# Routed experts of a decoder: the last row puts one per tile step, row loads 9 tiles ahead, and no order between the two

## The chip, the cores and the metric

The kernel runs on one core of a Trainium2 chip. A core has TensorE (PE in the profile; its weight loads are listed apart as PEld), VectorE (DVE), ScalarE (ACT), GpSimd (POOL) and SyncE (SP), each with a queue of its own that it works off in order, and 16 DMA engines that all of them share. The metric is the device time of one execution in microseconds (us).

## The reference

Two decoder layers over 16 sequences of 256 tokens with 128 features, all in float32. Each layer is self-attention, cross-attention to a context of 64 rows per sequence, and a mixture of experts. The change concerns the mixture of layer 0:

```python
logits = xn @ router_w
probs = jax.nn.softmax(logits, axis=-1)
topv, topi = jax.lax.top_k(probs, K)
topv = topv / jnp.sum(topv, axis=-1, keepdims=True)
comb = jnp.sum(jax.nn.one_hot(topi, E, dtype=xn.dtype) * topv[..., None], axis=1)
out = jnp.zeros_like(xf)
for e in range(E):
    out = out + comb[:, e:e + 1] * _swiglu(xn, gate_up_w[e], down_w[e])
out = out + _swiglu(xn, shared_gate_up_w, shared_down_w)
```

There are 4096 tokens, E = 8 experts and K = 2 choices per token. `xn` is the layernormed input. An expert is `silu(clip(gate)) * up @ down` with a hidden width of 512.

## The kernel before, in words

**Rows.** The kernel computes only the two experts that a token has chosen. The 4096 tokens are handled as 8 chunks of 512 (four blocks of 128). When the router has chosen for a chunk, every token gets two slots in a table of rows in device memory, `rows_in`, in which each expert has a region of its own. `p_pos` (L817) works the slots out on VectorE and writes them to `slot_in` (L826). `p_put` (L828) then scatters 128 rows of 130 numbers with one indirect DMA from POOL's queue (L830): two per block, eight per chunk, 64 in all.

**Tiles.** The experts' work is done in 71 tiles of 128 rows (NTILE). Of these, 41 (EARLY) are known to be full from the counts of the first six chunks alone (EARLY_C = 6); their table `tab_a` is made as soon as chunk 5 is routed. The other 30 come from `tab_b`, which is made when chunk 7 is routed. A tile needs its rows (`fetch`, L1313, a DMA from SP's queue into one of ROWS_AHEAD buffers `xr`), its expert's gate and up weights (`weights`, L1323, 512 KB from ACT's queue), a transpose on TensorE (`turn`, L1337) and its copy on ScalarE (`turned`, L1341), the matmuls `g` and `u` (`hidden`, L1369, eight lines each in the profile), a clip on VectorE and a silu on ScalarE (`gated`, L1376 and L1377), a product (`product`, L1381), the matmuls `y` (`down`, L1387, eight lines), a copy (L1396), and an indirect DMA from POOL that scatters the results to `rows_out` (`store`, L1397).

**Order.** Layer 0's self-attention comes first, as 134 steps (`steps`), two to an iteration of its loop. The cross-attention and the routing of each chunk (`front_pieces`, L601) are cut into small pieces, and `plan` (L1079) hangs piece k of chunk c on step 16c + 22 + k. A piece is a part for TensorE and a part for the other engines. The pieces of chunks 6 and 7 reach beyond step 134 and are worked off in the loop over tiles, where step 134 + i is tile step i: chunk 6's slots are made in tile step 7, chunk 7's in step 23. In a tile step i the program emits, in this order: the weights of tile i+6, the rows of tile i + ROWS_AHEAD, one of 20 weight loads for later layers (`pending`, L1428, from step 4 on), `turn(i+1)`, `hidden(i)`, TensorE's parts of the pieces, `down(i-2)`, `turned(i+1)`, `gated(i)`, the pieces' other parts, `targets(i)`, `product(i)` and `store(i-2)`.

In the attention the order on TensorE, VectorE, ScalarE and POOL is the order written in the program; the puts of chunks 0 to 5 have places there (`put_at`, L1119 on). In the loop over tiles it is written for TensorE, VectorE, ScalarE and SP:

```python
with tc.manual_schedule(engines=ordered | {mybir.EngineType.SP}):
```

POOL is not in that set: a planner puts POOL's instructions in an order by when it reckons that they are ready, the earlier emitted one first.

**Who waits for whom.** Puts and loads go to the same table `rows_in`, and a load's address is known only at run time, so a load waits for every put emitted before it, and a put waits for every load emitted before it, unless the program declares that two of them do not depend on each other. It does so for puts among themselves. One piece of a chunk's list, at L906, emits all eight puts of chunks 6 and 7 in one step, and is empty for the others:

```python
(None, lambda: None if c < EARLY_C else [p_put(t) for t in range(TPC)]),
```

Of the kernel before, what the change touches and what calls it, by code (L numbers as in the profile page):

```python
# [22 lines left out]
P = 128  # L23
# [4 lines left out]
NCHUNK = T // CH  # L28
TPC = CH // P
# [3 lines left out]
NTILE = 2 * NT + E - 1  # L33


EARLY_C = 6
SHARED_LATE = (4, 5, 6, 7)
EARLY = -(-(2 * CH * EARLY_C - E * (P - 1)) // P)
LATE = NTILE - EARLY
# [24 lines left out]
def kernel(ctx: ExitStack, tc: tile.TileContext, a: dict, out: bass.AP):  # L64
    nc = tc.nc
# [31 lines left out]
    rows_in = tc.dram_tile([ROWS, W], F32, name="rows_in")  # L97
# [129 lines left out]
    slots = ctx.enter_context(tc.tile_pool(name="slots", bufs=1))  # L227
# [16 lines left out]
    with ExitStack() as ph:  # L244
# [319 lines left out]
        first = wpool.tile([P, E], F32, tag="first", name="first")  # L564
# [5 lines left out]
        full = fp.tile([P, E, T // P], F32, tag="full", name="full")  # L570
        tiles = fp.tile([P, EARLY, E], F32, tag="tiles", name="tiles")
# [5 lines left out]
        tab_a = fp.tile([1, 2, EARLY], I32, tag="tab_a", name="tab_a")  # L577
        tab_b = fp.tile([1, 2, LATE], I32, tag="tab_b", name="tab_b")
        puts, puts_of, tabled, room = [], {}, {}, {"m": ps_m}

        def front_constants():

# [43 lines left out]
        def front_pieces(c):  # L626
# [142 lines left out]
            def p_turned2():  # L769
                if c in SHARED_LATE and "pool" in late:  # L770
                    g["xT"] = shared_xT[c] = late["pool"].tile(
                        [P, CH], F32, tag=f"xT{c}", name=f"xT_{c}"
                    )
                else:
                    held("xT", (P, CH))
                nc.scalar.activation(g["xT"], g.pop("tp"), AF.Identity, bias=bet, scale=gam)
                if c in SHARED_LATE and "pool" not in late:
                    shared_rows[c] = tc.dram_tile([P, CH], F32, name=f"xT_rows_{c}")
                    nc.sync.dma_start(shared_rows[c], g["xT"])
# [48 lines left out]
            def p_put(t, ks=(0, 1)):  # L828
                for k in ks:
                    put = nc.gpsimd.indirect_dma_start(  # L830
                        out=rows_in,
                        out_offset=bass.IndirectOffsetOnAxis(
                            slot_in[:, k, t0 + t : t0 + t + 1], 0
                        ),
                        in_=g["xn2"][:, t, :], in_offset=None,
                    )
                    for other in puts:
                        tc.declare_no_dep(
                            put.ins, other.ins, reason="slots of tokens are all different"
                        )  # L840
                    puts.append(put)


            def mm_sgate():
# [29 lines left out]
            def p_sdown():  # L874
# [28 lines left out]
            puts_of[c] = [lambda t=t, k=k: p_put(t, (k,)) for t in range(TPC) for k in range(2)]  # L903
            return [
                *first_part,
                (None, lambda: None if c < EARLY_C else [p_put(t) for t in range(TPC)]),  # L906
                *([] if c in SHARED_LATE else [
                    (mm_sgate, p_sgate),
                    (mm_sup, p_sup),
# [7 lines left out]
        def mm_counts(tiles_seen):  # L917
            ps = tabled["ps"] = room["m"].tile(
                [P, E], F32, tag="m", name=f"counts_{tiles_seen}"
            )  # L920
            nc.tensor.matmul(ps, ones, seen[:, tiles_seen, :], start=True, stop=True)
# [57 lines left out]
        def early_pieces():  # L979
# [13 lines left out]

            return [(lambda: mm_counts(EARLY_C * TPC), table), (None, table2)]

# [31 lines left out]
        with tc.manual_schedule(engines=ordered | {mybir.EngineType.Pool}):  # L1027
# [32 lines left out]
            got = [first_stats(t0) for t0 in (0, 2)]  # L1060
# [16 lines left out]
            side = {}  # L1077

            def plan(first, pieces):  # L1079
                for k, piece in enumerate(pieces):  # L1080
                    side.setdefault(first + k, []).append(piece)

            plan(17, [(lambda h=h: ctx_turn(h), lambda h=h: ctx_turned(h)) for h in range(2)])
            for c in range(NCHUNK):
                first_step = 16 * c + 22
                plan(first_step, front_pieces(c))
                if c == EARLY_C - 1:
                    plan(first_step + 24, early_pieces())
                if c == NCHUNK - 1:
                    plan(first_step + 25, late_pieces())  # L1090
# [7 lines left out]
            steps = n + 6  # L1098
# [7 lines left out]
            put_at = {}  # L1106
            for c in range(EARLY_C):
                for j, put in enumerate(puts_of[c]):
                    step = 8 * c + 23 + (j if c < EARLY_C - 1 else j // 4)
                    put_at.setdefault(step, []).append(put)  # L1110
# [189 lines left out]
    with ExitStack() as ph:  # L1300
# [4 lines left out]

        state, stores = {}, []
        room["m"] = ps_m
        AHEAD, ROWS_AHEAD = 8, 13

        def entry(i):  # L1310
            return (tab_a, i) if i < EARLY else (tab_b, i - EARLY)

        def fetch(i):  # L1313
            tab, k = entry(i)
            r = nc.values_load(
                tab[0:1, 1, k : k + 1], engines=[mybir.EngineType.SP], min_val=0,
                max_val=ROWS - P,
            )
            xr = fp.tile([P, W], F32, tag="xr", name=f"xr_{i}", bufs=ROWS_AHEAD)
            nc.sync.dma_start(xr, rows_in[bass.ds(r, P), :])  # L1320
            state.setdefault(i, {})["xr"] = xr

        def weights(i):  # L1323
# [86 lines left out]

        plan(steps + EARLY + 4, [(None, piece) for piece in strip_pieces()])
        plan(steps + NTILE, [(None, both)])
        assert 16 * (NCHUNK - 1) + 22 + 28 - steps <= EARLY - ROWS_AHEAD and max(side) - steps <= NTILE
        with tc.manual_schedule(engines=ordered | {mybir.EngineType.SP}):
            for i in range(AHEAD - 1):
                weights(i)
            for i in range(ROWS_AHEAD):
                fetch(i)
# [137 lines left out]
    with ExitStack() as ph:  # L1556
# [230 lines left out]
        with tc.manual_schedule(engines=ordered):  # L1787
# [55 lines left out]
            def shared_sum(c):  # L1843
                nc.gpsimd.tensor_tensor(x[c], x[c], shared_of.pop(("y", c)), ALU.add)
# [46 lines left out]
            plan = [w.split(":") for w in PLAN.split()]  # L1891
            plan = [(tok, int(lag)) for tok, lag in plan]
# [50 lines left out]
    with ExitStack() as ph:  # L1943
# [289 lines left out]
        plan = [part.split(":") for part in PLAN.split()]  # L2233
        with tc.manual_schedule(engines=ordered | {mybir.EngineType.Pool}):
            for word in (
# [6 lines left out]
                part, c = word.split(":")  # L2242
# [5 lines left out]
            for word in (  # L2248
# [12 lines left out]
                part, c = word.split(":")  # L2261
# [60 lines left out]
```

## Time and profile before

| What | Value |
|---|---|
| time, median of 5 runs | 1408.45 us (1406.52 to 1409.42) |
| the profiled execution's own time | 1410.43 us |
| its span, first to last instruction | 1408.5 us |
| mean granted TensorE clock | 0.981 |
| stage of the tiles | about 566 to 820 us |
| puts of rows (L830) | 64, of which 16 in the tile stage, from 621.2 to 692.0 us |
| stores of results (L1397) | 71, median 957 ns each on POOL |
| row loads (L1320) | 71, 65 KB each; the first 13 are issued from 575.75 us on, 1.13 us apart |

How to read it. The page gives one profiled execution. "Busy" is the share of the span in which an engine executes; instructions that only wait, branch, load a register or issue a DMA are not counted, except that POOL's indirect DMAs are shown for the time in which POOL prepares them, not for the transfer. In an order of time a line is: start, duration, engine, line of the kernel, operation, output <- inputs, shape, count, and in brackets how long the engine had been idle before and what ended that. "Issue" means that the engine waited for nothing that the profile shows; "remote", that the release came from something that the profile can't place. Times in the text without a unit are us from the start of the span. The granted clock is the share of full speed that TensorE's throttle gave.

### The profile page before, as it was taken

The numbers are of one execution on the slowest core, as the hardware profiler recorded it, in microseconds if no ns is written. First come the engines' busy times: TensorE is split into PE (matmuls) and PEld (weight loads), VectorE is DVE, ScalarE is ACT, GpSimd is POOL, SyncE is SP. The second block draws the span as 40 slices with busy tenths as digits, with TensorE's granted clock in tenths as the row PEclk, the third lists the DMA queues.
The fourth block names the chain that finished last, engine by engine and source line by source line (L and its number), as shares of the span: only waits on it lengthen the run. The fifth ranks groups of instructions, "written<-read, shape, count | busy, mean of one in ns | idle before, by whom it ended". The sixth has DMA issues, their size and how long they took to land.

```text
span 1408.5 us, 37939 instructions
## 1 busy us (share of the span) xinstructions
PE 1340.9 (95%) x13205; PEld 1002.7 (71%) x13205; DVE 1108.2 (79%) x4483; ACT 942.6 (67%) x2532; POOL 733.6 (52%) x1153
## 2 busy tenths in 40 slices
PE   9999999999999999899899989999999987899998
PEld 7777777777777776689799966666666654566665
DVE  5776877777777778657678769999999977888874
ACT  6776767667676766344233349999999984776662
POOL 6463648475756656643433373553334315677651
PEclk9999999999999999999899999999999998999998
DMA  6773000000000000557577420000000000122122
GB/s 161 233 243 86 2 6 9 9 9 9 7 11 7 17 9 23 174 178 236 177 244 233 162 77 17 17 17 10 17 3 2 2 2 1 32 54 61 39 59 63
DMA packets 80349, 95.86 MB, mean 68 GB/s; under 512 B 19568, under 2 KB 62832, under 8 KB 80160
## 3 DMA queue, kind: packets, MB, share of 16 engines
q1 hardware_dynamic: 65328, 46.25, 12.1%
q10 hardware_dynamic: 10512, 38.28, 8.0%
q0 software_dynamic: 4320, 8.92, 1.9%
q8 instruction: 106, 1.74, 0.5%
q14 instruction: 83, 0.68, 0.2%
HBM read 64.24 MB, written 29.17 MB: 66 GB/s over the span
## 4 chain that ended last, share of the span: by engine, by line
PE 66%; ACT 17%; DVE 10%; issue 3%; DMA 2%; POOL 1%; SPq 0%; POOLq 0%; ACTq 0%; DVEq 0%
ACT p L1730 8%; PE pqk L414 8%; PE o L546 5%; PE s L469 5%; PE u L1369 4%; PE g L1369 4%; PE y L446 4%; PE y L1387 4%; PE t L524 4%; PE pv L431 3%; PE t L1748 3%; PE o L1772 2%; ACT pT L1759 2%; PE s L1708 2%; PE g L2149 2%
## 5 line engine op out<-in xcount | busy, mean ns | idle before, releaser
L508 POOL TENSOR_SCALAR p<-p,rs 128x128 f32<-128x128 f32 (+1 forms) x512 | 213.4, 431 | 166.4 <-DVE rs L502 124.4
L494 ACT ACTIVATE p<-p,nm 128x128 f32<-128x128 f32 (+1 forms) x512 | 226.4, 447 | 24.7 <-DVE nm L482 20.6
L1730 ACT ACTIVATE p<-p,nm 128x256 f32<-128x256 f32 x512 | 220.7, 507 | 1.7 <-DVE nm L1719 0.4
L1719 DVE CUSTOM_DVE_ANT_0 p<-s,strip 128x256 f32<-128x256 f32 x512 | 186.7, 419 | 15.2 <-PE s L1708 14.5
L533 DVE COPY pT<-t 128x384 f32<-128x384 f32 x256 | 130.1, 549 | 39.2 <-PE t L524 37.7
L482 DVE CUSTOM_DVE_ANT_0 p<-s,strip 128x128 f32<-128x128 f32 (+1 forms) x512 | 154.0, 347 | 0.5 <-PE s L469 0.2
L1397 POOL DMA_INDIRECT rows_out<-yr,to x71 | 68.4, 964 | 121.5 <-DVE yr L1396 115.6
L1748 PEld LDWEIGHTS t<-ident,p 64*128 64x128 f32 x2048 | 80.4, 140 | 54.5 <-issue 16.1
L546 PEld LDWEIGHTS o<-pT,v 128*64 128x64 f32 x1024 | 64.2, 138 | 66.4 <-issue 34.1
L425 ACT ACTIVATE k<-pqk 128x512 f32<-128x512 f32 x64 | 38.1, 596 | 108.2 <-PE pqk L414 108.2
L1748 PE MATMUL t<-ident,p 64*128 64x64 f32 x2048 | 102.9, 232 | 7.9 <-ACT pT L1759 2.4
L1377 ACT ACTIVATE gs<-gs 128x512 f32<-128x512 f32 x71 | 44.7, 630 | 88.0 <-DVE gs L1376 76.6
L469 PE MATMUL s<-k,q 64*128 64x128 f32 (+1 forms) x1024 | 100.4, 332 | 0.3 <-DVE nm L482 0.3
L546 PE MATMUL o<-pT,v 128*64 128x256 f32 (+1 forms) x1024 | 99.0, 335 | 0.6 <-DVE pT L533 0.6
L494 ACT ACTIVATION_READ_ACCUMULATOR p<-p,nm 128x1 f32 x512 | 98.1, 192 | 0.0
L524 PE MATMUL t<-ident,p 64*128 64x64 f32 x1536 | 81.6, 228 | 14.0 <-ACT pre L737 4.7
L524 PEld LDWEIGHTS t<-ident,p 64*128 64x128 f32 x1536 | 68.5, 139 | 35.7 <-POOL p L508 8.7
L1708 PE MATMUL s<-k,q 32*128 32x256 f32 x1024 | 86.8, 410 | 1.4 <-DVE nm L1719 1.4
L1759 ACT COPY pT<-t 128x512 f32<-128x512 f32 x144 | 81.1, 587 | 6.8 <-PE t L1748 5.9
L440 DVE COPY v<-pv 128x512 f32<-128x512 f32 x64 | 44.2, 690 | 50.6 <-PE o L546 28.0
L1369 PE MATMUL u<-xTs,gu 128*128 128x128 f32 x568 | 77.9, 279 | 5.0 <-issue 5.0
L1387 PE MATMUL y<-dn,hT 128*128 x568 | 77.6, 280 | 3.0 <-issue 1.9
(365 smaller groups left out, 3355.0 us busy)
## 6 DMA issues: line engine op xcount, KB each, us to landing
gu<-in_L_ffn_gate_up_w ACTq DMA_DIRECT2D x71, 512.0 KB
rows_in<-zero SPq DMA_DIRECT2D x131, 130.0 KB
spread<-wrows SPq DMA_DIRECT2D x16, 512.0 KB
xr<-rows_in SPq DMA_DIRECT2D x71, 65.0 KB
y<-rows_out SPq DMA_DIRECT2D x16, 256.0 KB
out_x<-yo SPq DMA_DIRECT2D x16, 128.0 KB
x<-in_x SPq DMA_DIRECT2D x7, 256.0 KB
rows_out<-yr,to POOLq DMA_INDIRECT x71
```

The costliest lines, as they stand in the source:

```text
L469: nc.tensor.matmul(ps_of[b, h][:, cols], q[rows, u2, iq], k[rows, u2, 0:nk], start=True, stop=True,)
L482: nc.vector.tensor_tensor_reduce(out=pr[:, cols], in0=ps[:, cols], in1=strip[:, h, P : 2 * P] if it == 0 else strip[:, h, :], scale=1.0, s ...
L494: nc.scalar.activation(pr[:, cols], pr[:, cols], AF.Exp, bias=nm[:, it : it + 1], scale=-1.0, accum_out=sm[:, it : it + 1],)
L508: nc.gpsimd.tensor_scalar(pr[:, cols], pr[:, cols], rs[:, it : it + 1], 1.0, ALU.mult, ALU.mult)
L524: nc.tensor.transpose(halves[r][:, i, blk, :], pr[rows, blk * P : (blk + 1) * P], ident[rows, rows],)
L533: nc.vector.tensor_copy(pT_of[u][:, :, :, r, :], tp_of[u][r])
L546: nc.tensor.matmul(po[rows, c0:N], v[:, jt, h % 8 * DH : (h % 8 + 1) * DH], pT[:, 0:N] if jt == 0 else pT[:, N:], start=(jt == 0), stop=(j ...
L1369: nc.tensor.matmul(ps[:, f, :], gu[:, lo + f * P : lo + (f + 1) * P], xT, start=True, stop=True,)
L1387: nc.tensor.matmul(ps, s["hT"][:, f, :], dn0[:, bass.ds(s["e"], 1), f, :].rearrange("p e d -> p (e d)"), start=(f == 0), stop=(f == NF0 - 1),)
L1719: nc.vector.tensor_tensor_reduce(out=pr[:, it, :], in0=ps[:, it, :], in1=strip1[:, h, (1 - it) * P : (1 - it) * P + N], scale=1.0, scalar= ...
L1730: nc.scalar.activation(pr[:, it, :], pr[:, it, :], AF.Exp, bias=nm[:, it : it + 1], scale=-1.0)
L1748: nc.tensor.transpose(halves[r][:, k, jt, it, :], pr[rows, it, jt * P : (jt + 1) * P], ident[rows, rows],)
```

## The change

Four edits, all around the rows of layer 0's experts. The piece that emitted a chunk's eight puts at once is taken out of the list. For chunks 6 and 7 the eight puts are planned one per step instead, behind the chunk's last piece: tile steps 8 to 15 and 24 to 31. For chunks 0 to 3 the piece was empty; with it gone, their three pieces of the shared expert come one step earlier. Rows are loaded 9 tiles ahead, not 13, so there are 9 buffers `xr`. And each load of an early tile (i < EARLY) and each put of chunks 6 and 7 are declared not to depend on each other, whichever is emitted first. The assertion now asks that the last put is emitted before the first load that still depends on it, that of tile 41.

```diff
@@ p_put
                     puts.append(put)
+                    if c >= EARLY_C:
+                        late_puts.append(put)
+                        for other in early_fetches:
+                            tc.declare_no_dep(
+                                put.ins, other.ins, reason=APART,
+                            )
@@ front_pieces
             return [
                 *first_part,
-                (None, lambda: None if c < EARLY_C else [p_put(t) for t in range(TPC)]),
                 *([] if c in SHARED_LATE else [
@@ the plan
-                plan(first_step, front_pieces(c))
+                front = front_pieces(c)
+                plan(first_step, front)
+                if c >= EARLY_C:
+                    plan(first_step + len(front), [(None, put) for put in puts_of[c]])
+                    last_put = first_step + len(front) + len(puts_of[c]) - 1
@@ the tiles
-        AHEAD, ROWS_AHEAD = 8, 13
+        AHEAD, ROWS_AHEAD = 8, 9
@@ fetch
-            nc.sync.dma_start(xr, rows_in[bass.ds(r, P), :])
+            got = nc.sync.dma_start(xr, rows_in[bass.ds(r, P), :])
+            if i < EARLY:
+                early_fetches.append(got)
+                for other in late_puts:
+                    tc.declare_no_dep(got.ins, other.ins, reason=APART)
@@ the loop over tiles
-        assert 16 * (NCHUNK - 1) + 22 + 28 - steps <= EARLY - ROWS_AHEAD and max(side) - steps <= NTILE
+        assert last_put + 1 - steps <= EARLY - ROWS_AHEAD and max(side) - steps <= NTILE
```

`APART` is the reason given: the tiles of the first table are full of rows of the chunks that it counts, and rows of later chunks have slots behind those.

More of the change, by code (lines that the diff above doesn't have):

```diff
@@ L36 @@
 EARLY_C = 6
+APART = (
+    "the tiles of the first table are full of rows of the chunks that it counts, and rows of later"
+    " chunks have slots behind those"
+)
 SHARED_LATE = (4, 5, 6, 7)
@@ L579 @@
         puts, puts_of, tabled, room = [], {}, {}, {"m": ps_m}
+        late_puts, early_fetches = [], []
         def front_constants():
@@ L841, in p_put @@
                     puts.append(put)
+                    if c >= EARLY_C:
[3 more added lines that the diff above has]
+                                put.ins, other.ins, reason=APART,
+                            )
             def mm_sgate():
```

## The prediction

> **What bounds the kernel now.** I read the page first (who is busy, which slices lose clock), then busy time by stretches over the stage of the experts' tiles (566 to 820 us), then the order of time of POOL and of TensorE where a stretch falls out, then the waits there.
>
> ```profile
> span 1408.5 us, 37939 instructions
> PE 1340.9 (95%) x13205; PEld 1002.7 (71%) x13205; DVE 1108.2 (79%) x4483; ACT 942.6 (67%) x2532; POOL 733.6 (52%) x1153
> ```
>
> TensorE is busy 95% of the span: time is to be had only where it is not. Stretches of the tile stage (columns: length, busy us of PE, PEld, DVE, ACT, POOL, granted clock, DMA share, GB/s):
>
> ```profile
> 620.00:640.00 20.00, 16.65 (x106) 14.17 (x106) 7.66 (x23) 5.97 (x11) 11.81 (x13) 0.83 0.49 151
> 640.00:660.00 20.00, 20.00 (x182) 20.00 (x181) 17.19 (x56) 9.18 (x19) 9.34 (x11) 1.00 0.81 250
> 680.00:702.00 22.00, 15.39 (x105) 13.99 (x104) 12.59 (x49) 4.32 (x9) 11.59 (x12) 0.77 0.46 144
> 702.00:722.00 20.00, 20.00 (x181) 20.00 (x181) 15.35 (x46) 8.01 (x15) 7.62 (x8) 1.00 0.78 251
> ```
>
> Two stretches are bad: 106 matmuls where 182 go, clock at 0.83 and 0.77, and the DMA engines idler than beside them. What they have in common is POOL's queue (order of time, first stretch):
>
> ```profile
> 619.08 0.96 POOL L1397 DMA_INDIRECT rows_out<-yr,to  x1 [1.21 <-DVE yr L1396]
> 621.20 0.96 POOL L830 DMA_INDIRECT rows_in<-xn,slot_in  x1 [1.15 <-DMA xr<-rows_in]
> 622.46 0.95 POOL L830 DMA_INDIRECT rows_in<-xn,slot_in  x1 [0.30 <-issue]
> ...
> 630.03 0.96 POOL L830 DMA_INDIRECT rows_in<-xn,slot_in  x1 [0.30 <-issue]
> 631.29 0.96 POOL L1397 DMA_INDIRECT rows_out<-yr,to  x1 [0.30 <-issue]
> 632.55 0.96 POOL L1397 DMA_INDIRECT rows_out<-yr,to  x1 [0.30 <-issue]
> ```
>
> The eight puts (L830) stand back to back, one every 1.26 us, once the first has waited for a row load; the stores they held up (L1397) follow at the same pace. From 682.10 to 695.78 it is eight puts and three stores. TensorE in that second burst:
>
> ```profile
> 687.21 0.27 PE L1337 MATMUL xTr<-ident,xr 128*128 128x128 f32 x1
> 689.08 1.22 PE L1369 MATMUL g<-xTs,gu 128*128 128x128 f32 x8 [1.60 <-issue]
> 691.35 0.37 PE L1369 MATMUL u<-xTs,gu 128*128 128x128 f32 x1 [1.05 <-issue]
> 692.05 0.37 PE L1369 MATMUL u<-xTs,gu 128*128 128x128 f32 x1 [0.33 <-issue]
> 693.47 0.37 PE L1369 MATMUL u<-xTs,gu 128*128 128x128 f32 x1 [1.04 <-issue]
> ...
> 700.01 0.42 PE L1337 MATMUL xTr<-ident,xr 128*128 128x128 f32 x1
> ```
>
> The matmuls of `u` have their operands and need no one, yet they come 0.7 or 1.4 us apart (eight take 1.06 us elsewhere). The others wait for TensorE though it has done its part:
>
> ```profile
> ACT gs L1377 <- DVE gs L1376: 28.5, 13, 9.4
> DVE gs L1376 <- remote: 13.7, 2, 8.3
> ACT xTs L1341 <- remote: 5.7, 1, 5.7
> ```
>
> "Remote" is a release that the profile can't place: the clip of `g` starts at 635.40 and 697.72, while the `g` it reads ended at 625.93 and 685.59. So in a dense burst TensorE's signals come late, then its own issue slows down. Both times everything is released 1.9 us after the burst's last indirect DMA ends (633.51 and 695.78). That the dense run is the cause is my reading; the rows show only that they coincide, and that nothing like it stands elsewhere: stores 2.18 us apart (700.35, 702.53, 704.72) harm nothing.
>
> **What the two bursts cost.** From transpose to transpose (L1337) a tile step is 2.79 us. In burst 1 the transposes are at 624.77 and 635.95: 11.18 us, of which 2.79 is the step and 3.2 the gate's matmuls of chunk 7 (626.66 to 629.9), so 5.2 are lost; the next step, at half clock, takes 4.62, so 1.8 more. Burst 2: 687.21 to 700.01 is 12.80, so 10.0 lost, and 3.37 for the next, 0.6 more. Sum 7.0 + 10.6 = 17.6 us. No single step can give more than about that.
>
> **The change, part by part.**
>
> *Puts apart (L906 goes, L1086 adds them).* The number stays: 16 indirect DMAs, 0.96 us each and 0.30 between. What moves is their place on POOL's queue. POOL is not among the engines whose order is written out in this stage: what is ready early goes first there. The norm of chunk 7 (L670), emitted in step 7, ran at 610.67, ahead of the store of step 6 at 613.89; the two mixes (L742, L750) of steps 12 and 13 ran at 637.80 and 639.04 ahead of the store of step 11. So eight puts emitted over eight steps need not run over eight steps.
>
> *Puts and early loads don't wait for each other (declared).* In the old order it was this wait that held the puts to 621.20 and 682.10. Their slots are written by
>
> ```profile
> L826 DVE CAST slot_in<-slot x2: 170/170/171, 615.1 to 674.3; 128x8 int32<-128x8 f32 x2
> ```
>
> so all eight can go from 615.3 and 674.5. Between two stores (2.79 us apart, 1.26 each) stands 1.53 us of free POOL: room for one put, or for two with the store late. I take two per step as likeliest: put, put, store is 3.78 us of POOL in a step of 2.79, dense again, but every third operation is now a store that needs a result of TensorE. When signals lag, POOL meets a store that is not ready and pauses, and the pause ends the lag. The lag begins with the third or fourth dense operation (VectorE's L715 waits until 626.15 for a matmul that ended at 623.84). Eight puts and four or five stores give two such pauses; a pause lets go 1.9 us after the last operation, and with a matmul group restarted at part clock I put 2 to 3 us of TensorE on it: an estimate, 5 us per burst, 10 in all of the 17.6. Gain 7.6. Ends: all 17.6 gone; or the whole dense run charged (rival 3), 7.3 lost. I take the middle since the order is between the two rows it is nearest to, the burst (1.26 us apart) and the stores (2.18).
>
> The wait of SP's row load for the puts goes too (its issue stood from 617.99 to 633.22). It cost nothing: the row loaded then is read at 664.2.
>
> *Rows 9 tiles ahead, not 13.* Load i is issued when tile i-9 frees its buffer and read 8 steps on, 22.3 us; the load issued at 633.22 landed by 634.63, 1.4 us. At the start four loads of 1.13 us leave SP's head; tile 9 is read at 614.4, its buffer comes free at 592. Zero; if it were late, each us would be a us of TensorE. The first load that still waits for the late puts is tile 41's, in step 32, for a put issued in step 31 at the latest; SP's wait ended 3.2 us after the last put began (630.03 to 633.22), against 22.3. Behind it on SP stand only more row loads: the 20 weight loads of `pending` are out by step 23. Zero.
>
> *Puts ahead of chunk 7's mixes on POOL.* L742 and L750 (1.27 us each) may stand behind two indirect DMAs, 2.5 us, and VectorE waits for them in order. In the old order L742 waited idle 4.3 us for ScalarE, so I book 0, with 2.5 as the bad end.
>
> *The empty piece that goes for chunks 0 to 3.* Their shared expert's three pieces come one step earlier in the attention. Same matmuls (1.1 us for `sg`); now they cost a wait of 0.24 us (L524 at 272.84 for the clip L851), and a wait of 0.69 stands beside them for the gate's evacuation (286.05). Between -4 x 0.24 and +4 x 0.69 = -1.0 to +2.8; I take 0, as the next chunk's pieces that they now meet are lighter in one step and heavier in the other.
>
> **Row against rule.** The row says that a burst of indirect DMAs holds TensorE. The Trainium skill, page SBUF — State Buffer, section "SBUF: two separate sides", says that a DMA cannot be slowed by a compute operation or the other way round, the one trap being descriptors that GpSimd can't write while VectorE holds a shared port. By that rule the puts' spacing gives nothing and the time stays 1408.5. In this trace the puts keep their 1.26 us, so that trap is not what is seen, and TensorE does slow down beside them; I go by the row.
>
> **Sum.** The profiled execution took 1410.43 us, span 1408.5 and 1.93 around it; it lies 1.98 above the median 1408.45 (1406.52 to 1409.42). 1410.43 - 7.6 = 1402.8; against the median, 1400.9. **Predicted 1401 us**, 1396.5 to 1405.5 for this case alone.
>
> **Rivals.**
> 1. *One put per step, as emitted.* Store and put are 2.52 us of 2.79, POOL pauses in each step. For it: the pair at 640.46 and 641.75 harmed nothing (the clip at 641.77 follows `g` at 641.73, steps stay 2.79). Against: POOL's habit of running what is ready. Loss left about 2: gain 15.6, 1393.
> 2. *The burst only moves.* All eight are ready at once, and if nothing is ready between them they run back to back from 615.3 and 674.5, six to eight us earlier. Then the loss is as now, 17.6 give or take 3: 1405.5 to 1411.4. That TensorE's stall has another cause gives the same.
> 3. *Slower: no pauses.* If the stores are always ready when POOL comes to them, 8 puts and 5 stores run dense for 13 x 1.26 + 1.9 = 18.3 us. In burst 2 10.6 of 15.6 us were lost, 68%; of 18.3 that is 12.4, twice 24.9 against 17.6: +7.3, 1415.8. It decides from where TensorE's results lie a full store ahead of POOL through the burst. Against it: in burst 2 the store after the backlog waited 4.56 us for its result (700.35).
>
> **How the numbers follow.** Main case 0.35, rival 1 0.27, rival 2 0.20, rival 3 0.18. 0.2% is 2.8 us, about what a measurement of this kernel can tell from no change: faster means below 1405.6. Faster takes the main case but a little, and rival 1: 0.60; same is nearly all of rival 2: 0.19; slower is rival 3 and rival 2's upper end: 0.21. The range 1392 to 1412 leaves out the best of rival 1 and most of rival 3.
>
> **What would show it.** Right: L830 no longer in runs of eight but broken by L1397; granted clock above 0.9 and some 150 or more matmuls per 20 us where it was 106; the "remote" waits of L1376 under 3 us; no wait of L1337 for `xr`. Rival 1: no clock below 1.00 after 600 us. Rival 2: eight L830 in a row from 615 and 675. Rival 3: L830 and L1397 mixed with 0.30 between all, and transposes over 10 us apart. Wrong altogether: TensorE's slow issue at the same place without a dense run on POOL.

## The result and the profile after

| | time, median | ratio to before, 95% interval |
|---|---|---|
| before | 1410.06 us (1403.89 to 1414.20, 70 runs) | |
| after | 1412.26 us (1411.20 to 1415.86, 38 runs) | 1.0019 [1.0013, 1.0025] |

The change made the kernel slower by 0.19%, some 2.7 us: little, but clear of no change by the interval, where a gain of 7.6 us had been predicted. The profiled execution has a span of 1412.6 us against 1408.5, at the same mean clock (0.981).

The same stretches of the tile stage as in the prediction, in the kernel after (length, busy us of PE, PEld, DVE, ACT, POOL, granted clock, DMA share, GB/s):

```profile
620.00:640.00 20.00, 14.46 (x82) 12.27 (x82) 7.22 (x22) 6.36 (x10) 9.63 (x11) 0.74 0.51 141
640.00:660.00 20.00, 20.00 (x172) 18.95 (x171) 14.64 (x46) 7.62 (x14) 9.64 (x10) 1.00 0.64 200
680.00:702.00 22.00, 15.98 (x103) 14.62 (x103) 13.16 (x52) 4.81 (x9) 11.52 (x12) 0.77 0.51 162
```

Both holes are still there. The first is deeper (82 matmuls where it was 106, clock 0.74 where it was 0.83), the second is the same (103 and 105 matmuls). POOL in order of time shows why. L835 is the put, L1415 the store:

```profile
617.79 0.97 POOL L835 DMA_INDIRECT rows_in<-xn,slot_in  x1 [0.58 <-DVE at L1365]
...
620.34 0.96 POOL L835 DMA_INDIRECT rows_in<-xn,slot_in  x1 [0.30 <-issue]
621.60 0.96 POOL L1415 DMA_INDIRECT rows_out<-yr,to  x1 [0.30 <-issue]
622.87 0.96 POOL L835 DMA_INDIRECT rows_in<-xn,slot_in  x1 [0.30 <-issue]
...
627.93 0.96 POOL L1415 DMA_INDIRECT rows_out<-yr,to  x1 [0.31 <-issue]
629.20 0.95 POOL L835 DMA_INDIRECT rows_in<-xn,slot_in  x1 [0.30 <-issue]
633.94 0.96 POOL L1415 DMA_INDIRECT rows_out<-yr,to  x1 [3.79 <-DVE yr L1414]
```

Three puts, a store, four puts, a store, a put: ten operations, one every 1.26 us, with no pause. The two stores in the middle had their results before POOL reached them (0.30 of idle time, "issue"); the only pause (3.79) stands behind the last put. VectorE made these two results early in the burst:

```profile
618.59 0.28 DVE L1414 COPY yr<-y 128x128 f32<-128x128 f32 x1
620.77 0.28 DVE L1414 COPY yr<-y 128x128 f32<-128x128 f32 x1
```

The second burst has the same order from 680.62 to 692.96. TensorE's waits in it look as they did before (order of time):

```profile
686.30 0.36 PE L1387 MATMUL u<-xTs,gu 128*128 128x128 f32 x1 [0.28 <-issue]
687.72 0.27 PE L1387 MATMUL u<-xTs,gu 128*128 128x128 f32 x1 [1.06 <-issue]
...
693.33 0.37 PE L1405 MATMUL y<-dn,hT 128*128 x1 [1.03 <-issue]
694.76 0.45 PE L1355 MATMUL xTr<-ident,xr 128*128 128x128 f32 x1 [1.05 <-issue]
```

**Where the 4.1 us of the profiled span came from.** I set the start of every attention iteration and of every tile's transpose against the same one of before. The attention loses 0.57 to 0.66 us in each of chunks 0 to 3, where the shared expert's pieces moved up by a step, 2.2 us together at the first transpose. Burst 1 loses 3.1 more than it did (steps of 11.86 and 7.81 us where they were 11.18 and 4.62), burst 2 0.1 more, and 1.4 come back later. (Two later profiles of the changed kernel, in sets C and D below, show 1.6 more in burst 1 and 0.5 and 0.6 less in burst 2: 1.0 for both together, where it is 3.2 here.) The attention's loss is this wait, TensorE's flips (`t`) in chunk 0, in order of time, after:

```profile
200.19 0.27 PE L528 MATMUL t<-ident,p 64*128 64x64 f32 x1
201.34 0.58 PE L528 MATMUL t<-ident,p 64*128 64x64 f32 x11 [0.88 <-DVE gs L875]
```

and before:

```profile
199.30 0.27 PE L524 MATMUL t<-ident,p 64*128 64x64 f32 x1
199.81 0.58 PE L524 MATMUL t<-ident,p 64*128 64x64 f32 x11 [0.24 <-DVE gs L851]
```

The flips waited 0.24 us for the shared expert's clip; now the next piece (`su`) meets them, and they wait 0.88 us for its evacuation (L875): 0.64 us, four times. (Two line numbers in the description of the kernel before are off: `front_pieces` begins at L626, `put_at` at L1106.)

### The profile page after: what moved, and what is told of

It is laid out like the page before. It is cut to its first block, busy times and chain, and to the rows that moved or that the text cites. A ratio compares the mean times of both kernels' runs of the same rounds, so it can differ in the third digit from the quotient of the medians.

```text
span 1412.6 us, 37948 instructions
## 1 busy us (share of the span) xinstructions
PE 1343.1 (95%) x13205; PEld 1005.1 (71%) x13205; DVE 1108.0 (78%) x4483; ACT 943.0 (67%) x2532; POOL 736.9 (52%) x1153
## 4 chain that ended last, share of the span: by engine, by line
PE 68%; ACT 17%; DVE 11%; issue 2%; POOL 2%; DMA 1%; POOLq 0%; ACTq 0%; SPq 0%; DVEq 0%
ACT p L1748 8%; PE pqk L418 7%; PE s L473 5%; PE o L550 5%; PE g L1387 5%; PE u L1387 5%; PE y L1405 5%; PE y L450 4%; PE t L528 4%; PE t L1766 3%; PE pv L435 3%; PE o L1790 2%; PE s L1726 2%; ACT pT L1777 2%; PE g L2167 2%
## 5 line engine op out<-in xcount | busy, mean ns | idle before, releaser
L498 ACT ACTIVATE p<-p,nm 128x128 f32<-128x128 f32 (+1 forms) x512 | 226.5, 447 | 24.4 <-DVE nm L486 19.9
L1737 DVE CUSTOM_DVE_ANT_0 p<-s,strip 128x256 f32<-128x256 f32 x512 | 186.8, 419 | 15.7 <-PE s L1726 14.2
L1415 POOL DMA_INDIRECT rows_out<-yr,to x71 | 68.6, 966 | 124.9 <-DVE yr L1414 119.3
```

Of the source, the lines that this page charges most:

```text
L498: nc.scalar.activation(pr[:, cols], pr[:, cols], AF.Exp, bias=nm[:, it : it + 1], scale=-1.0, accum_out=sm[:, it : it + 1],)
L1737: nc.vector.tensor_tensor_reduce(out=pr[:, it, :], in0=ps[:, it, :], in1=strip1[:, h, (1 - it) * P : (1 - it) * P + N], scale=1.0, scalar= ...
```

## The experiments

There are five sets of runs. Each set ran on one chip, with runs of the kernel before beside it, and each on another chip. It turned out that the sets differ: before took 1410.9, 1410.9 and 1409.2 us in the sets called A, C and D here, and 1398.0 and 1399.5 us in B and E; the first table is like A, C and D. No chip had two of these sets, so whether the chip makes the difference, or something else that differed between the sets, is not shown. All ratios are within a set.

**Theories at the start.** *Density*: four or more indirect DMAs back to back on POOL hold TensorE, wherever they stand; the change moved them without thinning them out, and the empty piece adds 2.3 us. *Place*: TensorE stalls at chunk 6's and 7's late pieces for a reason of its own, and the DMAs only coincide.

### Set A: the empty piece, and the puts thinned out or gone

*The empty piece put back*, the rest of the change kept:

```diff
                 *first_part,
                 *([] if c in SHARED_LATE else [
+                    (None, lambda: None),
                     (mm_sgate, p_sgate),
```

> The changed kernel with the empty piece put back for chunks 0 to 3, so that the shared expert's pieces stand where they stood; puts, row loads and declarations as changed. Theory 'shift': the 2.2 us by which the first transpose of the tile stage is later (589.7 against 587.5) come from these pieces alone, 0.64 us in each of four chunks. Then the attention's iterations lie on those of before, and the time falls by 2.2 to 2.6 us against the changed kernel, to about 1410, the same as before. Rival 'POOL or row loads': the attention stays 2.2 us late, 1412.

Measured: 1409.67 us, ratio 0.9988 [0.9978, 0.9999]. Every attention iteration starts within 0.06 us of its time before: the shift is the whole of that loss. Both stalls stand: the tile stage is 2.5 us longer than before's.

*Each late put tied to its own tile step.* VectorE copies the put's slots in the put's step, so POOL can't run it earlier:

```diff
+                    where = slot_in[:, k, t0 + t : t0 + t + 1]
+                    if c >= EARLY_C:
+                        now = fp.tile([P, 1], I32, tag="now", name=f"now_{c}_{t}_{k}", bufs=8)
+                        nc.vector.tensor_copy(now, where)
+                        where = now[:, 0:1]
...
-                        out_offset=bass.IndirectOffsetOnAxis(
-                            slot_in[:, k, t0 + t : t0 + t + 1], 0
-                        ),
+                        out_offset=bass.IndirectOffsetOnAxis(where, 0),
```

> As the run with the piece back, and in addition each late put takes its slots from a small copy that VectorE makes in the put's own tile step (16 copies more, about 0.17 us each on VectorE, which is not the bound). So POOL's order is put, store, put, store, one put per step. Theory 'density': runs of indirect DMAs 1.26 us apart are what holds TensorE; without them no transpose comes over 5 us after the one before except in the step with the gate's matmuls (6.0), the granted clock stays 1.00 from 600 to 800 us, and 15 to 17 of the 17.6 us are gained: 1393 to 1396, ratio 0.989 to 0.991. Rival 'place': the stall belongs to these tile steps, whatever POOL's order: transposes over 10 us apart in steps 11 to 13 and 28 to 31, 1410. Between them: average spacing of 1.4 us is still dense, part of the loss stays in each of 16 steps, 1400 to 1408.

Measured: 1398.01 us, ratio 0.9912 [0.9896, 0.9928], 12.4 us faster. POOL now alternates and pauses (order of time; L840 is the put, L1419 the store):

```profile
619.30 0.97 POOL L840 DMA_INDIRECT rows_in<-xn,now  x1 [0.30 <-issue]
620.58 0.96 POOL L1419 DMA_INDIRECT rows_out<-yr,to  x1 [0.30 <-issue]
621.84 0.96 POOL L840 DMA_INDIRECT rows_in<-xn,now  x1 [0.30 <-issue]
625.63 0.96 POOL L1419 DMA_INDIRECT rows_out<-yr,to  x1 [2.83 <-DVE yr L1418]
```

and TensorE, in the two stretches:

```profile
620.00:640.00 20.00, 19.47 (x159) 17.35 (x158) 11.31 (x37) 8.52 (x15) 12.29 (x13) 1.00 0.75 192
...
680.00:702.00 22.00, 19.32 (x162) 18.08 (x161) 16.21 (x64) 7.16 (x13) 12.27 (x13) 1.00 0.68 193
```

Same number of puts and bytes in the same steps of the program, and both holes are gone but for a few steps of 3.1 to 4.3 us. In the profile the tile stage gains 9.9 of the 12.9 us; the step with the gate's matmuls (6.3 us) is nearly as long in the next kernel (6.2).

*No late puts at all*: the floor. This kernel leaves out the rows of chunks 6 and 7, and fills the table of results with zeros at the start instead.

```diff
+        for r in range(0, 2 * T, 2 * P):
+            nc.sync.dma_start(
+                rows_out[r : r + 2 * P, :].rearrange("(p r) d -> p r d", p=P), zero[:, :, 0:D]
+            )
...
-                    plan(first_step + len(front), [(None, put) for put in puts_of[c]])
+                    plan(first_step + len(front), [(None, lambda: None) for put in puts_of[c]])
```

> As the run with the piece back, without the 16 puts of chunks 6 and 7 (their rows are left out; the table of results is filled with zeros at the start instead, 32 more plain DMAs beside the 132 that fill the rows' table). It bounds what the late puts cost at all. Theory 'density': both stalls are gone, 17 to 18 us less than before, 1392 to 1394; if the alternating order gains as much, spacing alone does it. Rival 'place': 1410 with both stalls.

Measured: 1390.0 us, ratio 0.9853 [0.9834, 0.9872]. The tile stage gains 15.6 us on before, and the stretches are full:

```profile
620.00:640.00 20.00, 20.00 (x168) 18.23 (x167) 13.37 (x38) 8.10 (x15) 7.35 (x8) 1.00 0.69 188
680.00:702.00 22.00, 21.09 (x184) 20.67 (x185) 17.91 (x56) 8.71 (x16) 7.76 (x9) 1.00 0.82 244
```

The late puts' pieces otherwise ran as in the change, so *place* falls in this form; the next kernel makes stalls elsewhere. The rest of the gain (some 4 us of the profile) lies behind the tile stage and comes without the late puts gone, too: the kernel with the empty piece put back, which has all of them and both stalls, gains 4.1 us there. Its granted clock is 1.00 from 1120 to 1160 us, where before's is 0.91. Why the clock differs there is not shown.

*Added runs of puts of 2, 3, 4, 6 and 8* in the kernel before, in quiet tile steps, into a table that nobody reads:

```diff
+            def burst(n):
+                now = fp.tile([P, 2, TPC], I32, tag="now", name=f"now_{n}", bufs=2)
+                nc.vector.tensor_copy(now, slot_in[:, :, t0 : t0 + TPC])
+                for j in range(n):
+                    put = nc.gpsimd.indirect_dma_start(
+                        out=scratch,
+                        out_offset=bass.IndirectOffsetOnAxis(now[:, j % 2, j // 2 : j // 2 + 1], 0),
+                        in_=g["xn2"][:, j // 2, :], in_offset=None,
+                    )
...
+                    for at, size in ((36, 2), (41, 3), (46, 4), (52, 6), (59, 8)):
+                        plan(steps + at, [(None, lambda size=size: burst_of[NCHUNK - 1](size))])
```

> The kernel before, with five more runs of indirect DMAs of chunk 7's rows into a scratch table that nobody reads, in quiet tile steps: 2 in step 36, 3 in step 41, 4 in step 46, 6 in step 52, 8 in step 59. Theory 'density': 2 and 3 cost nothing, 4 under 2 us, 6 some 3 to 6 us, 8 some 8 to 11 us with the clock at half behind it, and TensorE's matmuls stand apart with nothing to wait for in the longer ones; the step is 2.79 us else. Rival 'place': all steps stay 2.79 us.

Measured: span 1431.7 us. The loss of each run, read as the jump in the transposes' starts against before:

| puts in the run | 2 | 3 | 4 | 6 | 8 |
|---|---|---|---|---|---|
| us lost | 0.07 | 0.9 | 5.1 | 7.3 | 10.3 |

Stalls appear wherever a run is put, and they grow with its length, from a step between three and four puts (the store that follows makes a dense run one longer). *Density* holds in this set.

### Set B: a set in which nothing was held

*One gated put in every second step.* From the version with gated puts:

```diff
-                    plan(first_step + len(front), [(None, put) for put in puts_of[c]])
-                    last_put = first_step + len(front) + len(puts_of[c]) - 1
+                    for j, put in enumerate(puts_of[c]):
+                        last_put = first_step + len(front) + min(2 * j, 13)
+                        plan(last_put, [(None, put)])
...
-        AHEAD, ROWS_AHEAD = 8, 9
+        AHEAD, ROWS_AHEAD = 8, 3
```

> The version with each late put gated by a VectorE copy in its own tile step, but one put in every second step (chunk 6 in tile steps 8 to 22, chunk 7 in 24 to 37, the last two in neighbouring steps), so POOL's order becomes put, store, store; rows are loaded 3 tiles ahead to leave room for it. Theory 'density' (four or more indirect DMAs on POOL 1.26 us apart hold TensorE, fewer don't): no run of four is left, the tile stage comes within 2 us of the kernel without late puts, time about 1392 (1390 to 1395), ratio 0.987. Rival 'each late put costs a fixed sum while the tiles run' (in the kernel with one put per step 16 puts cost 5.7 us beyond the kernel without them, 0.36 each): 1398, ratio 0.991, as there. Rival 'rows 3 ahead are too few' (a load lands about 2 us after its issue, 3 steps are 8.4 us): waits of the row transpose on its load appear, time over 1398.

Measured: 1430.23 us, ratio 1.0223 [1.0199, 1.0246]. The third expectation came true: three tiles ahead are too few. Waits from 590 to 850 us:

```profile
PEld xTr L1360 <- DMA xr<-rows_in: 15.7, 14, 3.1
PE xTr L1360 <- DMA xr<-rows_in: 15.6, 17, 2.9
```

A buffer comes free only late in a tile step, so three tiles ahead are two steps of time or less. This kernel says nothing on the puts.

*Rows 9 ahead alone*, in the kernel before:

```diff
-        AHEAD, ROWS_AHEAD = 8, 13
+        AHEAD, ROWS_AHEAD = 8, 9
```

> The kernel before with one part of the change alone: rows loaded 9 tiles ahead in place of 13. The prediction's term: 0. Every theory held now: the same within 0.2%, ratio 0.998 to 1.002, the two stalls where they were before. Rival 'fewer rows in flight expose the wait of SP on the late puts': steps beside the bursts longer, time 2 us or more above before.

Measured: 1399.47 against 1398.03 us, ratio 1.0002 [0.9985, 1.0019]. Nothing, as predicted, but the profile was another one. POOL ran the same ten dense operations (eight puts from 622.35, 1.26 us apart), and TensorE ran through them: 137 matmuls and clock 1.00 from 620 to 640 us where before's profile had 106 and 0.83. What was left of each burst is a wait further down. SyncE's queue waits, from 610 to 710 us:

```profile
SPq L1320 <- DMA rows_in<-xn,slot_in: 32.9, 2, 17.0
```

SyncE and then ScalarE, in order of time, at the first of the two:

```profile
617.72 0.34 SPq L1320 DMA_DIRECT2D xr<-rows_in  x1
618.10 0.49 SPq L1428 DMA_DIRECT2D wq_u<-in_L_xattn_wq  x1
635.67 0.35 SPq L1320 DMA_DIRECT2D xr<-rows_in  x1
...
637.35 0.34 SPq L1320 DMA_DIRECT2D xr<-rows_in  x1
```

```profile
633.17 0.63 ACT L1377 ACTIVATE gs<-gs 128x512 f32<-128x512 f32 x1 [1.12 <-DVE gs L1376]
639.32 0.41 ACTq L1330 DMA_DIRECT2D gu<-in_L_ffn_gate_up_w  x1
639.78 0.46 ACT L1341 ACTIVATE xTs<-xTr,bet,gam 128x128 f32<-128x128 f32 x1 [5.98 <-DMA xr<-rows_in]
```

SyncE's next row load stands from about 618.6 to 635.6 for the last put. The tile that it loads isn't needed for long, but ScalarE's next weight load (L1330) signals on the same semaphore as the row load issued at 637.35, so it is not issued before that one has landed (639.2). The copy of the transposed rows (L1341) stands behind it in ScalarE's queue, 5.98 us late, and TensorE behind that. The tile step is 7.88 us here and 6.87 at the second burst, 5.1 and 4.1 over 2.79.

*Five added runs of eight transfers of different kinds* in the kernel before (rows 11 ahead): whole rows, a quarter of the columns, a quarter of the rows, and plain transfers from POOL and from SyncE:

```diff
+                    if kind == "few_columns":
+                        put = nc.gpsimd.indirect_dma_start(
+                            out=narrow, out_offset=bass.IndirectOffsetOnAxis(where, 0),
+                            in_=rows[:, 0:32], in_offset=None,
+                        )
+                    elif kind == "few_rows":
+                        put = nc.gpsimd.indirect_dma_start(
+                            out=scratch, out_offset=bass.IndirectOffsetOnAxis(where[0:32, :], 0),
+                            in_=rows[0:32, :], in_offset=None,
+                        )
+                    elif kind == "plain_pool":
+                        put = nc.gpsimd.dma_start(straight[j * P : (j + 1) * P, :], copied)
+                    elif kind == "plain_sp":
+                        put = nc.sync.dma_start(straight2[j * P : (j + 1) * P, :], copied)
```

> The kernel before (rows 11 ahead) with five added runs of eight transfers of chunk 7's rows, each gated by a VectorE copy, in tile steps 36 (indirect, 128 rows x 130 columns), 42 (indirect, 128 x 32, a quarter of the bytes), 48 (indirect, 32 x 130, a quarter of the rows), 54 (plain DMAs issued by POOL, 128 x 130) and 60 (plain DMAs issued by SP, 128 x 130). The first repeats the known run of eight: 10 us lost, all theories. Theory 'POOL's work per row' (descriptors written by POOL): few columns loses 10 as well, few rows 0 to 2, plain from POOL up to 10, plain from SP 0. Theory 'bytes moved': few columns and few rows 0 to 2, both plain runs 10. Theory 'any indirect DMA instruction, whatever its size': few columns and few rows both 10, plain runs 0.

Measured: one run, 1402.91 us. No kind of run costs anything but the last (1.2 us), the eight whole puts included. The stretch of that first run:

```profile
715.00:745.00 30.00, 30.00 (x272) 30.00 (x270) 23.79 (x72) 11.52 (x21) 22.96 (x24) 1.00 0.81 241
```

So *density* alone is not the cause either: it takes a set in which it acts. From here the theory was *two causes*: where dense indirect DMAs hold TensorE, the hold covers SyncE's wait; where they don't, SyncE's wait is what a burst costs, and the change takes it away.

### Set C: the hold again

*The changed kernel once more:*

> The changed kernel itself, once more. In the last set of runs the kernel before took 1398.0 us and its traced relative (rows 9 ahead) had no step over 8 us in the tile stage: TensorE's signals kept pace with the puts, and what was left of each burst was one wait, of SP for a late put, with 32.9 us in two waits, behind which tile 16's and tile 34's row came late (steps 7.9 and 6.9). If this set is like that one, theory 'two causes' (TensorE held in some sets of runs; where it is not, SP's wait binds): the change, which takes SP's wait away, gains 7 to 9 us less the 2.3 of the left-out piece, about 1391 to 1393 against 1398, ratio 0.995 to 0.997. Rival 'the puts are simply hidden there': same, 0.999 to 1.002. If the set is like the first (before 1410), the known 1412, ratio 1.001 to 1.003, in both.

Measured: 1412.65 against 1410.94 us, ratio 1.0014 [1.0003, 1.0026]; steps of 11.88 and 10.83 us. The set is like A.

*The five kinds of run:*

> The same kernel with five added runs of eight transfers as in the last set, where none of them but the last (plain, from SP: 1.2 us) cost anything. If this set is one in which TensorE is held (before 1410): first run 10 us; theory 'POOL's work per row': few columns 10, few rows 0 to 2, plain from POOL up to 10, plain from SP about 1; theory 'bytes': few columns and few rows 0 to 2, both plain runs 10; theory 'any indirect DMA': few columns and few rows 10, plain runs 0 to 1. If it is not, all 0 to 1 as in the last set.

Measured: one run, 1440.3 us. Lost: 10.0 us (whole rows), 8.4 (a quarter of the columns), 10.3 (a quarter of the rows), 0 (plain, POOL), 0.6 (plain, SyncE). The stretches of the first three, in the same kernel that showed 272 matmuls in 30 us above:

```profile
715.00:745.00 30.00, 24.01 (x181) 23.44 (x180) 14.83 (x44) 7.89 (x15) 14.34 (x16) 0.83 0.56 175
745.00:770.00 25.00, 20.53 (x151) 19.23 (x150) 13.64 (x42) 6.14 (x12) 13.42 (x14) 0.86 0.51 161
770.00:800.00 30.00, 23.86 (x179) 22.68 (x179) 18.29 (x59) 8.00 (x15) 13.67 (x15) 0.83 0.53 160
```

Neither the bytes nor the rows count, it is the indirect DMAs as such, 1.26 us apart (1.17 with 32 rows). The plain ones from POOL cost nothing, but their run was over in 4.4 us (0.54 us each, back to back), no longer than the indirect run of three that cost 0.9; so for them this is not settled.

*Puts at two paces, rows 6 ahead:* chunk 6 one in two steps, chunk 7 two in three.

```diff
+                    for j, put in enumerate(puts_of[c]):
+                        last_put = first_step + len(front) + (2 * j if c == EARLY_C else 3 * j // 2)
+                        plan(last_put, [(None, put)])
...
-        AHEAD, ROWS_AHEAD = 8, 9
+        AHEAD, ROWS_AHEAD = 8, 6
```

> As the kernel with one gated put in every second step, but rows 6 ahead in place of 3 (chunk 6's puts in tile steps 8 to 22, one in two; chunk 7's in 24 to 34, two in three). With rows 3 ahead the row transpose waited for its load all through the tiles (time 1430). Theory: with 6 ahead a load is issued some 13 us early, no such wait is left, POOL has no run of four, and the time is near that of the kernel without late puts: 1391 to 1394 where before takes 1410 (ratio 0.987 to 0.989), 1388 to 1391 where it takes 1398 (0.993 to 0.995). Rival 'a fixed price for each late put': 1398 where before takes 1410. Rival 'rows ahead still too few': the transpose's waits on its load stay, time over 1400.

Measured: 1397.01 us (1392.58 to 1401.25), ratio 0.9894 [0.9866, 0.9921]. The transposes no longer wait for loads, but the time is not near the floor. The loss lies in one place: up to tile step 20 this kernel gains as much on before as the one without late puts (both 6.8 us, counted from the stage's start; chunk 6's puts go one in two steps), and between steps 21 and 38 it falls 7.7 us behind that one, where chunk 7's puts come two in three steps. POOL still has dense runs of four there (from 671.3, 695.0 and 702.1). So a late put has no fixed price, and "POOL has no run of four" was wrong for chunk 7.

*No late puts:*

> The kernel without the puts of the last two chunks (their rows, and what hangs on them, are missing from the output), once more: the floor that a placement of the puts can reach. 1390 where before takes 1410 (ratio 0.985). Where before takes 1398: theory 'two causes' 1387 to 1389 (the steps of 7.9 and 6.9 go, about 9 us, ratio 0.993); rival 'hidden' 1398.

Measured: 1391.04 us, ratio 0.9863 [0.9840, 0.9887]; the tile stage gains 15.7 us.

### Set D: the hold, and one part of the change alone

*Rows 9 ahead and no wait between early loads and late puts; the burst stays in one step and the empty piece stays.* Against the change:

```diff
                 *first_part,
+                (None, lambda: None if c < EARLY_C else [p_put(t) for t in range(TPC)]),
...
-                    plan(first_step + len(front), [(None, put) for put in puts_of[c]])
-                    last_put = first_step + len(front) + len(puts_of[c]) - 1
+                    last_put = first_step + len(front) - 1
```

> One part of the change alone: rows 9 ahead and no wait of early loads for the late puts; the puts stay in one step of eight as before and the empty piece stays. Where TensorE is held during the bursts (before 1410): theory 'the hold covers SP's wait' (SP's wait ends inside the hold): same within 0.2%, 1409 to 1412. Rival 'SP's wait binds in every set': 7 to 9 us faster. Where it is not held (before 1398): the steps of 7.9 and 6.9 behind SP's wait go, 1389 to 1391, ratio 0.993 to 0.995.

Measured: 1407.55 against 1409.21 us, ratio 0.9987 [0.9976, 0.9998]: the same within 0.2%. The two stalls stand (steps of 11.80 and 10.64 us). POOL's order in this kernel, which emits all eight puts in one step, is three puts, a store, five puts, a store: nearly that of the changed kernel. So planning the puts one per step did next to nothing to POOL's order.

*The gated puts, and the changed kernel:*

> The version with each late put gated in a tile step of its own, once more. Where TensorE is held (before 1410): ratio 0.991 as before. Where it is not (before 1398): no run to break up, but SP's wait is gone too, so 1389 to 1392, ratio 0.993 to 0.996.

> The changed kernel, a third time. Where TensorE is held (before 1410): 1412, ratio 1.001 to 1.003. Where it is not (before 1398): SP's wait is gone and the left-out piece costs 2.3, so 1391 to 1393, ratio 0.995 to 0.997.

Measured: 1396.65 us, ratio 0.9909 [0.9886, 0.9932]; and 1413.45 us, ratio 1.0028 [1.0016, 1.0041].

### Set E: no hold, and the change gains

> The changed kernel, a fourth time. Where TensorE is held (before 1410): 1412, ratio 1.001 to 1.003. Where it is not (before 1398): SP's wait is gone and the left-out piece costs 2.3, so 1391 to 1393, ratio 0.995 to 0.997.

> Rows 9 ahead and no wait of early loads for the late puts, the burst in one step, once more. Where TensorE is held (before 1410): the same within 0.2%, ratio 0.998 to 1.001, as in the last set (0.9987). Where it is not (before 1398): the two steps behind SP's wait go, 1389 to 1391, ratio 0.993 to 0.995.

Measured: before 1399.5 us, the changed kernel 1394.41, ratio 0.9970 [0.9954, 0.9985]; the part alone 1391.25, ratio 0.9941 [0.9921, 0.9960]. Both fall where *two causes* put them as a ratio. The changed kernel here, its stretches and what SyncE's queue waited for most (610 to 710 us):

```profile
620.00:640.00 20.00, 19.48 (x161) 17.57 (x160) 12.59 (x36) 9.80 (x16) 14.05 (x15) 1.00 0.74 210
...
680.00:702.00 22.00, 21.08 (x184) 20.42 (x183) 18.45 (x61) 8.70 (x16) 11.10 (x13) 1.00 0.79 253
```

```profile
SPq L1334 <- DVE at L1365: 52.6, 32, 4.5
```

The wait for puts is gone, the stretches are nearly as full as without late puts, and the tile stage is as short as there (15.7 us below that of before's profile). Yet POOL's order of the first burst is the very one that stalled 12 us in the profile after:

```profile
617.61 0.97 POOL L835 DMA_INDIRECT rows_in<-xn,slot_in  x1 [0.58 <-DVE at L1365]
...
628.99 0.96 POOL L835 DMA_INDIRECT rows_in<-xn,slot_in  x1 [0.30 <-issue]
630.25 0.96 POOL L1415 DMA_INDIRECT rows_out<-yr,to  x1 [0.30 <-DVE hT L1399]
```

Here POOL even goes on with stores without a pause, since TensorE keeps delivering. The changed kernel is 3.2 us slower than the part alone: 2.1 of it is the moved pieces (offset of the first transpose against before's profile, 2.07 to -0.01).

| | hold (A, C, D) | no hold (B, E) |
|---|---|---|
| before | 1409.2 to 1410.9 us | 1398.0, 1399.5 us |
| changed kernel | 1.0014, 1.0028 | 0.9970 |
| no wait of early loads, burst and empty piece as before | 0.9987 | 0.9941 |
| empty piece put back | 0.9988 | not run |
| each late put in its own step | 0.9912, 0.9909 | not run |
| puts at two paces | 0.9894 | not run |
| no late puts | 0.9853, 0.9863 | not run |

Where there is a hold, two versions beat both kernels by about 1%. Where there is none, the part alone does by 0.6%. Which of them is best in every set was not tried.

## Why the prediction was wrong

- **The step that failed: "Eight puts and four or five stores give two such pauses".** The interleaving came ("three puts, a store, four puts, a store, a put" is near "put, put, store"), the pauses did not. I had reasoned that when TensorE's signals lag, POOL meets a store that is not ready. But two stores had their results before POOL came to them (copied by 618.87 and 621.05, stored at 621.60 and 627.93), and POOL's planner had put just these two between the puts. Only the third store had to wait, and it stands behind the burst. So the dense run stayed ten long, and where I had left 10 us of the 17.6 lost, all of it was, and 1.0 to 3.2 more in the three profiles of the changed kernel that show the stalls. By its size this is the second rival, "the burst only moves"; by its signs it is the third, "no pauses": puts and stores mixed with 0.30 between all and transposes over 10 us apart, not eight puts in a row. Rival 3 had counted thirteen operations, and there were ten. The bursts began at 617.79 and 680.62, 0.3 and 0.8 us after the slots were written; the prediction's 615.3 and 674.5 are the times of the slots in before, 2.2 and 5.3 us earlier.
- **The size of the two holes (17.6 us) was nearly right**: without late puts the tile stage gains 15.6 and 15.7 us, 6.8 in burst 1 and 8.9 in burst 2. I had put 10.6 on burst 2, since I took 2.79 for both of its steps; without late puts they take 3.85 and 3.45. The time gains more (20.9 and 19.9 us); the rest shows up after the tile stage, as in a kernel that keeps both stalls.
- **Density as the cause: right in the sets that show the hold, and not the whole cause.** Added runs of puts stall TensorE anywhere, thinning them out gives 9.9 and 9.3 us of the tile stage, and in two of five sets dense runs do not stall it. What I drew from the rule of the Trainium skill (SBUF — State Buffer, "SBUF: two separate sides"), that spacing gives nothing, agrees with sets B and E. It fails in A, C and D, by 10 us a run of eight.
- **The empty piece, taken as 0, is a loss of 2.1 to 2.6 us**, inside its stated bounds of -1.0 and +2.8 and near the bad end. I had seen both waits (0.24 and 0.69 us) and said that one gets heavier and one lighter; the gate's wait stayed and the other grew by 0.64. With 2.3 for this term rival 2's 1405.5 to 1411.4 becomes 1407.8 to 1413.7, and the measured 1412.3 lies in it.
- **SyncE's wait, taken as 0: right under the hold** (0.9987), **wrong without it**, where it is worth some 8 us (1399.5 - 1391.25). The step "behind it on SP stand only more row loads" missed that a weight load of ScalarE waited for one of these row loads through a shared semaphore. The row of the late tile itself was early enough, as I had written.
- **Rows 9 ahead: right**, 1.0002, in the one set (B) where it ran alone.
- **Puts ahead of chunk 7's mixes: right as far as it shows.** Without a hold the changed kernel has no step over 3.9 us from tile step 14 on.

## What to carry to other kernels

An order that a planner makes is not the order of the program: to thin out a queue, tie each operation to something that is made in its own step, and read the queue in order of time. When a wait is called free, follow everything behind it, other queues that share its semaphore included, and ask whether it is free in itself or only covered by a larger stall. And compare kernels in more than one set, on more than one chip, before a stall is called a property of the kernel: here the sign of a 0.2 to 0.3% change differed between sets.

## What the runs showed of the hardware

Indirect DMAs from POOL at 1.26 us each hold TensorE in three sets of five, each on a chip of its own. Added runs lost 0.07 us with two of them, 0.9 with three, 5.1 with four, 7.3 with six and 10.3 with eight: one added run of each size, in set A. In set C runs of eight lost 10.0 us with whole rows, 10.3 with 32 rows instead of 128, and 8.4 with 32 columns instead of 130. The profile then shows engines that start long after the matmul they wait for (the clip of `g` at 635.40, `g` ended at 625.93 in before), matmuls 0.7 or 1.4 us apart, and an end some 2 us after the last indirect DMA. The ends of matmuls are modelled in the profile, so it does not tell a late signal from a late matmul. In the other two sets such runs did not stall TensorE: eight added ones cost nothing, nor do 24 in 30 us with the stores around them. What makes the difference between the sets, and what connects POOL's queue with TensorE, these runs do not show.
